# Pair attention: ScalarE's adds of two slots issued ahead of the next block's exponential, with another choice of ScalarE's five halves

## The chip, the cores and the metric

The kernel runs on one core of a Trainium2 chip. The time is the device time of one execution in microseconds (us). Before the change the median of three runs is 5141.64 us, and the runs lie between 5141.53 and 5143.81 us.

Five engines of the core matter here. TensorE (PE in the profile) multiplies matrices. VectorE (DVE), ScalarE (ACT) and GpSimd (POOL) work on elements. SyncE (SP) issues most of the transfers. Each engine takes its instructions strictly in the order in which the program lists them, and waits for the others through semaphores.

## What is computed

Two layers are computed one after the other, each an attention and a feed-forward network (FFN) with residuals and normalisation. The change touches the attention of the second layer alone. In the reference it is this:

```python
q = jnp.einsum('bnc,ac->bna', X, Wq)
k = jnp.einsum('bnc,ac->bna', X, Wk)
Vy = jnp.einsum('bnc,dc->bnd', X, Wy_w) + Wy_b
e = jax.nn.relu(_rho_signed_sqrt(q[:, :, None, :] + k[:, None, :, :]))
scores = jnp.einsum('bija,a->bij', e, Wphi)
m = jnp.max(scores, axis=-1, keepdims=True)
ex = jnp.exp(scores - m)
denom = jnp.sum(ex, axis=-1)
part1 = jnp.einsum('bij,bjc->bic', ex, Vy)
Ew = jnp.einsum('bij,bija->bia', ex, e)
part2 = jnp.einsum('bia,ca->bic', Ew, We_w) + We_b * denom[..., None]
```

The quantity `e`, which has an element for each query, key and one of 64 channels, is the large one. The relu of the signed root keeps only the root of the positive part, so the kernel computes it as a relu of the sum `q + k` and then a square root. It is needed twice, once for the scores and once more, weighted by `ex`, for `Ew`.

## The kernel before

**The tiling.** There are 4 batches of 1024 tokens. The queries are taken 32 at a time, which makes a *block*; there are 128 blocks (`N = B * NB`). A block consists of 8 *pairs*, numbered 0 to 7, and a pair of two *halves*, so that half i = 2 * pair + h runs from 0 to 15. One half is a tile of 128 partitions x 1024 keys. A pair is one buffer `s` of 128 x 2048, taken from a ring of 14 buffers (`RING`).

**What is done to a pair.** First each half gets its add: `max(k + q, 0)`. This is done on one of three engines: GpSimd for the halves in `ADD_ON_POOL` (line 1381, issued by `begin`), ScalarE for the halves in `RELU_ON_SCALAR` (line 1403, in `pair`), and VectorE for the others (line 1392, in `adds`). Then ScalarE takes the square root of the whole pair in place (line 1404), and TensorE adds the pair into the block's scores with 32 products (line 1408). When all 8 pairs are in, `top` takes a maximum on VectorE (line 1418), `quarters` (line 1420) and two products (line 1421) spread it, `exps` takes the final maximum on VectorE (`neg`, line 1425), and ScalarE computes the exponential (line 1427). `spread` copies the weights to all partitions with TensorE (line 1434, tile `xb`). At last VectorE multiplies each half by its weights and sums it, in `weigh` (line 1454); only then is the ring buffer free.

**The order.** It is written out by hand. The main loop goes over the blocks n and, inside, over 8 *steps* p. In step p VectorE weighs the two halves of pair p of block n, with the add of a pair that is 12 pairs ahead in between. After that come `top` of block n+1 (step 5), or `exps` and the first `spread` of block n+1 (step 6). Then `work` issues a share of other work, namely the first layer's remainder at the start, and later the second layer's FFN. At the end of the step a pair 14 ahead is begun (GpSimd's add) and a pair 12 ahead is made (`make`, which calls `pair`). So the step decides which pair is made:

| step p | pair made, of block n+2 (n+1 for p below 4) | ScalarE's halves before | VectorE's half before |
|---|---|---|---|
| 0 | 4 | 8 | - |
| 1 | 5 | - | 10 |
| 2 | 6 | 12 | - |
| 3 | 7 | 14 | 15 |
| 4 | 0 | - | 0 |
| 5 | 1 | 2 | - |
| 6 | 2 | - | 4 |
| 7 | 3 | 6 | 7 |

GpSimd has halves 1, 3, 5, 9, 11 and 13. So each engine's number of halves of a block is fixed: five on ScalarE, five on VectorE and six on GpSimd. While the first layer's remainder still runs (`first_rest`), the ring lends a buffer to it, and everything is one pair less ahead.

ScalarE must load another function table whenever it goes from the square root to the exponential and back. The FFN's own SiLU and GELU passes (line 1357, `between` and `switch`) are held back until directly after the exponential, so that they share a change of table. Their normalisation (lines 913 and 929, in `normed`) runs wherever `work` issues it.

Of the kernel before, what the change touches and what calls it, by code (L numbers as in the profile page):

```python
# [8 lines left out]
AF = mybir.ActivationFunctionType  # L9
# [22 lines left out]
PREP = 12  # L32
ROOM = (4, 6, 6, 6, 6, 4, 3, 6)
LATE = 2
RELU_ON_SCALAR = (2, 6, 8, 12, 14)
FIRST_ON_SCALAR = 6
ADD_ON_POOL = (1, 3, 5, 9, 11, 13)
LEAD = 2
# [5 lines left out]
@with_exitstack  # L44
def block_kernel(ctx: ExitStack, tc: tile.TileContext, a, out):
    nc = tc.nc
    keep = ctx.enter_context(tc.tile_pool(name="keep", bufs=1))


    kept = ctx.enter_context(tc.tile_pool(name="kept", bufs=1, space=DRAM))  # L50
    link = {
        "x1": [kept.tile([U, C], F32, tag=f"x1_{j}", name=f"x1_{j}") for j in range(B * T // U)],
        "x2": [kept.tile([FB, C], F32, tag=f"x2_{j}", name=f"x2_{j}") for j in range(B * T // FB)],
        "gates": [kept.tile([1, 2, B, C], F32, tag=f"gates{j}", name=f"gates{j}") for j in range(2)],
        "brow": kept.tile([1, C], F32, tag="brow", name="brow"),
        "yg": kept.tile([P, 4, U], F32, tag="yg", name="yg"),
        "qd": kept.tile([T, 64], F32, tag="qd0", name="qd0"),
        "kd": kept.tile([8, P, T], F32, tag="kd0", name="kd0"),
        "vd": kept.tile([T, C + 1], F32, tag="vd0", name="vd0"),
    }  # L60

    ident = keep.tile([P, P], F32, tag="ident", name="ident")
    nc.scalar.dma_start(ident, a["ident"])
    eps = keep.tile([P, 3], F32, tag="eps", name="eps")
    for i, v in enumerate((EPS_LN, EPS_GN, EPS_RHO)):
        nc.vector.memset(eps[:, i : i + 1], v)
    cols = [keep.tile([P, 6, 2, B], F32, tag=f"mcols{i}", name=f"mcols{i}") for i in range(2)]
    seen = keep.tile([P, NE], F32, tag="seen", name="seen")
    link["qt"] = [keep.tile([P, 64, 8], F32, tag=f"qt{i}", name=f"qt{i}") for i in range(2)]
    nc.gpsimd.memset(seen, 0.0)  # L70
    first_layer(tc, a, link, cols, seen, ident, eps)
    pair_attention(tc, a, link, out, cols, seen, ident, eps)
# [750 lines left out]
def pair_attention(tc, a, link, out, cols_of, seen, ident, eps):  # L823
# [10 lines left out]
    nc = tc.nc  # L834
    NB = T // 32
# [3 lines left out]
    with tc.tile_pool(name="at_k", bufs=1) as pk, tc.tile_pool(name="at_w", bufs=1) as wp, tc.tile_pool(  # L839
# [14 lines left out]
        kB, qtab, kds, vds = {0: {}}, {0: link["qt"][0]}, {0: link["kd"]}, {0: link["vd"]}  # L854
# [18 lines left out]
        for i in range(2):  # L873
            t = wp.tile([P, 4, P], F32, tag=f"ewt{i}", name=f"ewt{i}")
            nc.gpsimd.memset(t, 0.0)
            ewt.append(t)
            t = wp.tile([P, 4, 64], F32, tag=f"ew{i}", name=f"ew{i}")
# [379 lines left out]
        def follower():  # L1257

            return groups.get(stream[1]) if len(stream) > 1 else None
# [103 lines left out]
        class Block:  # L1363


            def __init__(self, n):
                self.n, self.b, self.s, self.added = n, n // NB, {}, set()
                self.sc = psc.tile([P, 512], F32, tag="sc", name="sc")

            def on_scalar(self, i):  # L1370
                return i in RELU_ON_SCALAR if self.n else i < FIRST_ON_SCALAR

# [3 lines left out]
            def begin(self, p):  # L1376
                self.s[p] = ring.tile([P, 2, T], F32, tag="s", name="s")
                for h in range(2):
                    i = 2 * p + h
                    if self.n and i in ADD_ON_POOL:  # L1380
                        nc.gpsimd.tensor_scalar(  # L1381
                            self.s[p][:, h, :], kB[self.b][i % 8], self.query(i), 0.0, ALU.add, ALU.max
                        )

            def adds(self, p):
# [3 lines left out]
                for h in range(2):  # L1389
                    i = 2 * p + h  # L1390
                    if not (self.n and i in ADD_ON_POOL or self.on_scalar(i)):
                        nc.vector.tensor_scalar(  # L1392
                            self.s[p][:, h, :], kB[self.b][i % 8], self.query(i), 0.0, ALU.add, ALU.max
                        )

            def pair(self, p):
                t = self.s[p]
                s = p // 4
                self.adds(p)
                for h in range(2):  # L1400
                    i = 2 * p + h
                    if self.on_scalar(i):
                        nc.scalar.activation(t[:, h, :], kB[self.b][i % 8], AF.Relu, bias=self.query(i))  # L1403
                nc.scalar.activation(t, t, AF.Sqrt, bias=eps_rho)  # L1404
                for h in range(2):
                    g = (2 * p + h) % 8
                    for j in range(4):
                        nc.tensor.matmul(  # L1408
                            self.sc[32 * j : 32 * j + 32, 0:256],
                            wsel[:, g, 16 * (1 - s) : 16 * (1 - s) + 32],  # L1410
                            t[:, h, 256 * j : 256 * (j + 1)],
                            start=p == 0 and h == 0,
                            stop=p == 7 and h == 1,
                        )
# [121 lines left out]
        N = B * NB  # L1536
        blocks = {0: Block(0)}
        begun = made = 0
# [3 lines left out]
        def work(room):  # L1542


            tick()
            turns[0] += 1
            if issues and turns[0] % 2:
                issues.pop(0)()
            for of in (tasks, stream):
                while of and room > 0:  # L1550
                    got = next(of[0], self_done)
                    if got is self_done:
                        of.pop(0)
                    elif got is None:
                        break
                    else:
                        room -= got
# [10 lines left out]
        def make():  # L1568
            nonlocal made
            n, p = made // 8, made % 8  # L1570
            if n < N:
                blocks[n].pair(p)
                if n % NB == NB - 1 and n + 1 < N and p >= 4:
                    for g in range(2 * p - 8, 2 * p - 6):
                        spread_keys(n // NB + 1, g)
            made += 1
# [13 lines left out]
        for n in range(N):  # L1590
            cur = blocks.pop(n)
            ew = ews[n // 4 % 2]
            if n % 4 == 0:
                exT = p2.tile([P, 4, 2, P], F32, tag="exT", name="exT")
            nxt = n + 1 < N
            if n % NB == PREP and n // NB + 1 < B:
                stream.insert(min(1 + (follower() in heads), len(stream)), prepare(n // NB + 1))
            for p in range(8):
                if p == 0:
                    cur.spread(1)  # L1600
                    cur.turn()
                if p == 2:
                    cur.turned(exT)
                cur.weigh(p, 0, ew)
                if made < 8 * N:
                    blocks[made // 8].adds(made % 8)
                cur.weigh(p, 1, ew)
                if nxt and p == 5:
                    blocks[n + 1].top()
                if nxt and p == 6:  # L1610
                    blocks[n + 1].exps()
                    blocks[n + 1].spread(0)
                work(ROOM[p])
                while begun <= 8 * n + p + ahead[0]:
                    begin()
                    make()
            if n % 4 == 3:
                tasks.append(finish(n, ew, exT))
# [104 lines left out]
```

## Time and profile before

| | |
|---|---|
| median of the three runs | 5141.64 us |
| the profiled execution, its own time | 5137.34 us |
| its span, first to last instruction | 5135.6 us |
| mean granted TensorE clock | 0.900 |
| first and last exponential of the attention (line 1427) start at | 1268.9 and 4968.3 us |
| GpSimd's adds (line 1381) | 762 x 3.792 us |
| VectorE's adds (line 1392) | 645 x 0.922 us |
| VectorE's weighing (line 1454) | 2048 x 1.209 us |
| scores on TensorE (line 1408) waiting for the square root, matmul rows | 402.5 us |
| VectorE's score maximum (line 1418) waiting for TensorE | 208.8 us |
| VectorE's weighing waiting for the spread weights (line 1434) | 33.7 us |

"Span" is the time between the first and the last instruction of the profiled execution; the execution's own time holds 1.7 us more. Durations are those of this one execution. The pages of the profile give, for each group of instructions, the busy time, the mean duration of one, and the idle time of the engine just in front of it with what ended it. Passes of ScalarE and VectorE overlap their predecessor by a little under 0.1 us, so starts, not durations, are subtracted where a rate is wanted.

The 128 exponentials divide the attention into 127 intervals. From block 28 on most of them fall into a pattern of eight that returns, because two groups of the FFN take eight blocks; eight copies of it run from block 28 to 51, 68 to 83 and 100 to 123. The copy from 4203.1 us (block 100) to 4430.5 us (block 108) is the one used for working things out.

### The profile page before, as it was taken

Reading aid. Unit: us, or ns where it says so; the run is one execution under the profiler, and the core shown is the slowest. Engines: PE = TensorE matmul, PEld = TensorE weight load, DVE = VectorE, ACT = ScalarE, POOL = GpSimd, SP = SyncE. Lnnn points to the kernel's source line nnn. Section 1 sums busy time; section 2 is a strip of 40 time slices with the busy share of each in tenths; the row PEclk is TensorE's granted clock in tenths of the full one; section 3 lists DMA queues with packets and bytes.
Section 4 is the critical chain, followed back from the end, with each engine's and each line's share of the span. In section 5 each row is a group of like instructions: output and inputs, shape, how many; then the busy total and the mean of one; then the engine's idle time right before and its main releaser. Section 6 shows DMA issues by size and latency. Waiting matters only on the chain.

```text
span 5135.6 us, 75609 instructions
## 1 busy us (share of the span) xinstructions
PE 4334.1 (84%) x28714; PEld 2437.5 (47%) x28714; DVE 4175.7 (81%) x7255; ACT 3690.1 (72%) x3438; POOL 3396.9 (66%) x1233
## 2 busy tenths in 40 slices
PE   6788888877688979888887988888889889798888
PEld 2233333333234635555554555555455556455557
DVE  5877777765799888888888888888888988988871
ACT  2322222213899889999998889999888999999961
POOL 3533343433688777787887778788867877887840
PEclk8798888988798989999898999999889999999999
DMA  4233333344011222222121323222223222121223
GB/s 137 85 101 105 96 97 89 88 115 117 18 36 58 82 86 87 98 74 83 61 73 51 118 76 111 69 78 71 72 72 108 99 77 80 62 79 66 73 82 114
DMA packets 255787, 429.16 MB, mean 84 GB/s; under 512 B 71752, under 2 KB 142592, under 8 KB 255168
## 3 DMA queue, kind: packets, MB, share of 16 engines
q1 hardware_dynamic: 251776, 420.76, 25.8%
q8 instruction: 227, 3.72, 0.3%
q10 hardware_dynamic: 3168, 1.99, 0.1%
q0 software_dynamic: 480, 1.57, 0.1%
q14 instruction: 136, 1.11, 0.1%
HBM read 396.13 MB, written 40.67 MB: 85 GB/s over the span
## 4 chain that ended last, share of the span: by engine, by line
PE 34%; ACT 18%; DVE 15%; issue 7%; POOL 1%; DMA 0%; ACTq 0%; POOLq 0%; SPq 0%; DVEq 0%
PE ff_ps L1315 14%; PE sc L1408 10%; DVE s L1454 9%; ACT s L1404 9%; ACT s L1403 4%; PE xb L1434 2%; DVE s L1392 2%; PE out_ps L1336 2%; PE o L1505 2%; ACT L1404 2%; ACT L1357 1%; PE o L1517 1%; PE ff_ps L1245 1%; ACT wide L1357 1%; ACT ex L1427 1%
## 5 line engine op out<-in xcount | busy, mean ns | idle before, releaser
L1381 POOL TENSOR_SCALAR s<-kB,qt 128x1024 f32<-128x1024 f32 x762 | 2879.7, 3792 | 603.6 <-DVE ew L1454 480.4
L1454 DVE CUSTOM_DVE_ANT_0 s<-s,xb 128x1024 f32<-128x1024 f32 x2048 | 2417.0, 1209 | 35.1 <-PE xb L1434 33.7
L1404 ACT ACTIVATE s<-s,eps 128x2048 f32<-128x2048 f32 x1024 | 2027.6, 2000 | 76.0 <-DVE s L1392 30.4
L1408 PE MATMUL sc<-s,wsel 128*32 128x256 f32 x16384 | 1198.5, 417 | 404.6 <-ACT s L1404 402.5
L1315 PE MATMUL ff_ps<-wide,fw 128*128 128x256 f32 x4096 | 1006.0, 395 | 29.2 <-ACT wide L1357 25.6
L1408 PEld LDWEIGHTS sc<-s,wsel 128*32 128x32 f32 x16384 | 456.2, 115 | 1006.9 <-ACT s L1404 600.3
L1315 PEld LDWEIGHTS ff_ps<-wide,fw 128*128 128x128 f32 x4096 | 765.7, 194 | 237.6 <-issue 99.5
L1403 ACT ACTIVATE s<-kB,qt 128x1024 f32<-128x1024 f32 x641 | 728.9, 1138 | 23.5 <-DMA yg<-out_g 22.8
L1392 DVE TENSOR_SCALAR s<-kB,qt 128x1024 f32<-128x1024 f32 x645 | 594.1, 922 | 0.4 <-DMA kB<-kd 0.4
L729 POOL TENSOR_TENSOR kv<-vb,out_k 128x512 f32<-128x512 f32 x256 | 323.1, 1270 | 285.5 <-DVE state L797 225.5
L607 PE MATMUL e_ps<-wd,hid 128*128 128x512 f32 x896 | 429.1, 626 | 34.0 <-DVE acc L590 33.2
L1434 PE MATMUL xb<-ex,pick 64*128 64x256 f32 x2048 | 324.9, 440 | 56.9 <-ACT ex L1427 56.9
L797 DVE TENSOR_TENSOR_SCAN state<-dec,carry,kv 128x512 f32<-128x512 f32 x256 | 325.9, 1273 | 9.9 <-POOL carry L792 5.0
L607 PEld LDWEIGHTS e_ps<-wd,hid 128*128 128x128 f32 x896 | 176.0, 202 | 281.0 <-issue 273.4
L1434 PEld LDWEIGHTS xb<-ex,pick 64*128 64x128 f32 x2048 | 195.4, 206 | 194.6 <-ACT ex L1427 96.8
L1245 PE MATMUL ff_ps<-wide,fw 128*128 128x256 f32 x1024 | 266.0, 409 | 6.1 <-ACT wide L929 5.8
L799 DVE TENSOR_TENSOR pr<-state,rec 128x512 f32<-128x512 f32 x256 | 176.0, 687 | 113.2 <-ACT state L795 66.5
L789 ACT COPY carry<-state 128x1 f32<-128x1 f32 x255 | 47.8, 187 | 263.9 <-DVE state L797 262.9
L1245 PEld LDWEIGHTS ff_ps<-wide,fw 128*128 128x128 f32 x1024 | 197.4, 202 | 64.9 <-issue 25.3
L1418 DVE TENSOR_REDUCE sc<-sc 128x1 f32<-128x256 f32 x128 | 54.9, 429 | 208.9 <-PE sc L1408 208.8
L1299 DVE TENSOR_TENSOR wide<-ff_ps,ffn_s 128x512 f32<-128x512 f32 x128 | 87.7, 685 | 167.7 <-PE ff_ps L1315 167.7
L1427 ACT ACTIVATE ex<-sc,neg 128x256 f32<-128x256 f32 x128 | 60.6, 473 | 201.0 <-DVE neg L1425 200.1
(254 smaller groups left out, 4002.8 us busy)
## 6 DMA issues: line engine op xcount, KB each, us to landing
fw<-in_ffw_dram SPq DMA_DIRECT2D x354, 512.0 KB
vb<-vd SPq DMA_DIRECT2D x1024, 64.0 KB
lent<-vd SPq DMA_DIRECT2D x64, 514.0 KB
wd<-in_w_down_dram SPq DMA_DIRECT2D x28, 1024.0 KB
kB<-kd SPq DMA_DIRECT2D x32, 512.0 KB
lent<-in_We_dram SPq DMA_DIRECT2D x32, 512.0 KB
kd<-nd SPq DMA_DIRECT2D x24, 512.0 KB
vd<-out_v SPq DMA_DIRECT2D x8, 512.0 KB
```

The costliest lines, as they stand in the source:

```text
L607: nc.tensor.matmul(ps, hid[:, k, t * P : (t + 1) * P], wd[:, k, :], start=k == 0, stop=k == HID // P - 1)
L729: nc.gpsimd.tensor_mul(kv, vb[:, g % 2, :], ready[u]["k"][:, n // HN, :])
L797: nc.vector.tensor_tensor_scan(s[:, 1 : U + 1], dec, kv, c, ALU.mult, ALU.add)
L1245: nc.tensor.matmul(ps[:, h, :], w[:, k, o : o + P], hT[:, k, :], start=k == 0, stop=k == 1)
L1315: nc.tensor.matmul(ps[:, h, :], w[:, k * P : (k + 1) * P], of[:, k, :], start=k == 0, stop=k == 7)
L1381: nc.gpsimd.tensor_scalar(self.s[p][:, h, :], kB[self.b][i % 8], self.query(i), 0.0, ALU.add, ALU.max)
L1392: nc.vector.tensor_scalar(self.s[p][:, h, :], kB[self.b][i % 8], self.query(i), 0.0, ALU.add, ALU.max)
L1403: nc.scalar.activation(t[:, h, :], kB[self.b][i % 8], AF.Relu, bias=self.query(i))
L1404: nc.scalar.activation(t, t, AF.Sqrt, bias=eps_rho)
L1408: nc.tensor.matmul(self.sc[32 * j : 32 * j + 32, 0:256], wsel[:, g, 16 * (1 - s) : 16 * (1 - s) + 32], t[:, h, 256 * j : 256 * (j + 1)], s ...
L1434: nc.tensor.matmul(xb[:, 256 * j : 256 * (j + 1)], pick[q, j % 2, s, :], self.ex[q, :], start=True, stop=True)
L1454: nc.vector.tensor_tensor_reduce(t[:, h, :], t[:, h, :], self.xb[s], 1.0, 0.0, ALU.mult, ALU.add, ew[:, self.n % 4, col : col + 1])
```

## The change

There are two edits. The first replaces the five halves that ScalarE adds: 2 and 6 leave the list, 4 and 7 enter it. VectorE takes 2 and 6 instead of 4 and 7, since it takes whatever neither of the others has. The second splits ScalarE's adds of a pair off into a function `relus`, which does them once, and calls it in step 6 for the pairs that are begun and not yet made, in front of `exps`. In the steady state those are the pairs made in steps 6 and 7, that is, halves 4 and 7; `pair` later finds them done.

```diff
-RELU_ON_SCALAR = (2, 6, 8, 12, 14)
+RELU_ON_SCALAR = (4, 7, 8, 12, 14)
...
+            def relus(self, p):
+                if p in self.relued:
+                    return
+                self.relued.add(p)
+                for h in range(2):
+                    i = 2 * p + h
+                    if self.on_scalar(i):
+                        nc.scalar.activation(self.s[p][:, h, :], kB[self.b][i % 8], AF.Relu, bias=self.query(i))
+
             def pair(self, p):
                 t = self.s[p]
                 s = p // 4
                 self.adds(p)
-                for h in range(2):
-                    i = 2 * p + h
-                    if self.on_scalar(i):
-                        nc.scalar.activation(t[:, h, :], kB[self.b][i % 8], AF.Relu, bias=self.query(i))
+                self.relus(p)
                 nc.scalar.activation(t, t, AF.Sqrt, bias=eps_rho)
...
                 if nxt and p == 6:
+                    for m in range(made, min(begun, 8 * N)):
+                        blocks[m // 8].relus(m % 8)
                     blocks[n + 1].exps()
                     blocks[n + 1].spread(0)
```

More of the change, by code (lines that the diff above doesn't have):

```diff
@@ L1366, in __init__ @@
             def __init__(self, n):
-                self.n, self.b, self.s, self.added = n, n // NB, {}, set()
+                self.n, self.b, self.s, self.added, self.relued = n, n // NB, {}, set(), set()
                 self.sc = psc.tile([P, 512], F32, tag="sc", name="sc")
```

## The prediction

> **What bounds the kernel now.** I read the page's busy shares and chain first, then its groups, then the waits of the exponential, then single blocks in order of time.
>
> ```profile
> PE 4334.1 (84%) x28714; PEld 2437.5 (47%) x28714; DVE 4175.7 (81%) x7255; ACT 3690.1 (72%) x3438; POOL 3396.9 (66%) x1233
> ...
> PE 34%; ACT 18%; DVE 15%; issue 7%; POOL 1%; DMA 0%; ACTq 0%; POOLq 0%; SPq 0%; DVEq 0%
> ```
>
> No engine is the bound. The chain that ended last changes engines: it runs on TensorE while the FFN's products fill it, on VectorE, and on ScalarE after an exponential. In the attention ScalarE is the fullest: from 2000 to 2500 us it is busy 455.5 of 500 us (TensorE 437, VectorE 435). What it still idles is mostly one wait:
>
> ```profile
> L1404 ACT ACTIVATE s<-s,eps 128x2048 f32<-128x2048 f32 x1024 | 2027.6, 2000 | 76.0 <-DVE s L1392 30.4
> ...
> L1403 ACT ACTIVATE s<-kB,qt 128x1024 f32<-128x1024 f32 x641 | 728.9, 1138 | 23.5 <-DMA yg<-out_g 22.8
> ...
> L1427 ACT ACTIVATE ex<-sc,neg 128x256 f32<-128x256 f32 x128 | 60.6, 473 | 201.0 <-DVE neg L1425 200.1
> ```
>
> The last row: 201 us idle in front of the exponential, in 78 of the 128 blocks; in the other 50 ScalarE came late itself. The wait is uneven: along the eight-block pattern (exponentials 101 to 108) it is 0, 2.07, 3.95, 0.47, 0, 4.64, 0 and 0 us. The change fills this hole. What counts is whether it was on the path, and what the filling does where there is no hole.
>
> **The change on ScalarE.** The adds are five per block before and after. Up to now, from exponential to exponential, ScalarE does roots 2, add 6, 3, add 8, 4, 5, add 12, 6, add 14, 7, 0, add 2, 1. Afterwards: roots 2, 3, add 8, 4, 5, add 12, 6, add 14, 7, 0, 1, then adds 4 and 7. By starts: root to root 1.91 us (4211.11 to 4213.02), root-add-root 3.07 (4204.90 to 4207.97) to 3.14, so an add between roots costs 1.16 to 1.23. Two adds in a row before the table load cost an estimated 1.04 each (1.13 less the 0.09 overlap). Hence: (a) 0.3 us less of ScalarE per block; (b) everything from root 3 to root 0 comes 1.16 us sooner after the exponential, root 1 by 2.4; (c) from root 1 to the exponential there are 2.1 us more, or 0.86 more counted from root 0.
>
> **The change on VectorE.** Its five adds stay, but one moves: half 4's in step 6, between score maximum and `neg`, goes; half 2's comes in step 5, ahead of the maximum. Where VectorE waits there for scores, the new add is free and the old one (0.67 to 1.6 us) leaves the path to `neg`. Otherwise they cancel. And root 1, which needed only ScalarE and GpSimd, now waits for VectorE's step 5. A block where this bites, ScalarE first, then VectorE:
>
> ```profile
> 4309.11 2.00 ACT L1404 ACTIVATE s<-s,eps 128x2048 f32<-128x2048 f32 x1 [1.05 <-DVE s L1392]
> 4311.02 1.13 ACT L1403 ACTIVATE s<-kB,qt 128x1024 f32<-128x1024 f32 x1
> 4312.24 2.00 ACT L1404 ACTIVATE s<-s,eps 128x2048 f32<-128x2048 f32 x1
> 4314.26 1.28 ACT L1427 ACT_TABLE_LOAD   x1
> 4316.01 0.47 ACT L1427 ACTIVATE ex<-sc,neg 128x256 f32<-128x256 f32 x1 [0.47 <-DVE neg L1425]
> ```
>
> ```profile
> 4310.07 1.21 DVE L1454 CUSTOM_DVE_ANT_0 s<-s,xb 128x1024 f32<-128x1024 f32 x1
> ...
> 4311.21 1.21 DVE L1454 CUSTOM_DVE_ANT_0 s<-s,xb 128x1024 f32<-128x1024 f32 x1
> ...
> 4312.35 0.42 DVE L1418 TENSOR_REDUCE sc<-sc 128x1 f32<-128x256 f32 x1
> ...
> 4314.02 0.75 DVE L1392 TENSOR_SCALAR s<-kB,qt 128x1024 f32<-128x1024 f32 x1
> ...
> 4315.82 0.15 DVE L1425 TENSOR_REDUCE neg<-sc 128x1 f32<-128x4 f32 x1
> ```
>
> The new add fits in at 4311.21 and ends at 4311.96. Root 1, two adds, load: 0.06 + 1.91 + 1.04 + 1.15 + 1.30 = 5.46, so the exponential could start at 4317.4 instead of 4316.01. `neg` stays (one add in, one out). The exponential is 1.4 to 1.6 us late, and what is queued behind it on ScalarE is late too: the FFN's wide pass and root 2, for which TensorE waits.
>
> **The table load against a rule.** The rows show 1.28 us, starting 0.02 after the pass in front, with the next pass 0.01 behind. [...]
>
> **GpSimd.**
>
> ```profile
> 4365.73 7.37 POOL L1381 TENSOR_SCALAR s<-kB,qt 128x1024 f32<-128x1024 f32 x2
> 4377.98 3.70 POOL L1381 TENSOR_SCALAR s<-kB,qt 128x1024 f32<-128x1024 f32 x1 [4.88 <-DVE ew L1454]
> ```
>
> The second pass of the first row is half 9 and ends at 4373.1, before pair 6 is weighed (4374.8): it took the buffer of pair 5. So a buffer goes to whichever pair is first written. With add 7 in front, pair 3 takes that buffer and half 9 waits for pair 6's: from 4369.4 to 4374.8. It then ends at 4378.5, root 4 needs it at about 4381.7; halves 11 and 13 follow at 4382.2 and 4385.9, and root 6 comes at 4387.0 (4388.18 less 1.16). The narrowest margin is 1.1 us, so I cost it at nothing; without it, root 6 waits for the excess. VectorE's moved add runs more often beside GpSimd (97% of blocks there, 81% before; adds beside it average 0.97 us, others 0.75). Bounds of an add: 0.74 to 1.70; I take 0.95. TensorE's products, the transfers and SP's queue are the same in number and order.
>
> **The sum for eight blocks** (shift of the path, us):
> - 100 to 101: ScalarE never idles: -0.3.
> - 101 to 102: root 2, TensorE, then VectorE to `neg`; add 0.95 for 0.70: +0.25. The 2.07 wait just holds two adds.
> - 102 to 103: TensorE throughout: 0. The 3.95 us hole is filled for nothing.
> - 103 to 104, 105: +1.5 as above. TensorE later waited 0.72 for root 7, which now comes sooner, so +0.8 remains.
> - 105 to 106: TensorE, then VectorE's maximum after 2.65 us of waiting; the add behind it (1.59 long) goes: -1.5.
> - 106 to 107: ScalarE again: -0.3.
> - 107 to 108: the path comes by the FFN's normalisation, which ScalarE ends at 4426.04. Then add, root, load was 4.55 to the exponential; root, add, add, load is 5.40: +0.86.
>
> That is -0.2 in 227 us, or -1.5 for the eight copies. By the same steps 60 to 68 and 92 to 100 give -0.5, -0.7, -0.3, -0.7, +1.0, thus -1.2 each; 12 to 27, 52 to 59 and 84 to 91 about +1 (five times -0.7 and five times -0.3 against 1.6, 0.6 and four times 0.86); the first eleven blocks -0.3 each, -3 (an add out of the run up to the last root, 1.16, one in before `neg`, 0.75 to 0.95). Together -6 us. The profiled execution's 5137.3 becomes 5131; the median stands 4.3 above it, so **5136 us** is forecast: gains and losses cancel. About 0.2%, 10 us, is what a measurement tells from no change.
>
> **Rivals.**
> - *The hole was on the path.* Then each waiting block gains up to one add: the smaller of 1.13 and its wait sums to 78 us. For it: 50 of the 78 waits are on the chain. Against: after the longest waits the chain goes on over TensorE, where an earlier root 3 buys nothing. 50/78 of it is 50 us: 5092.
> - *The exponential becomes the late one (slower).* Place: blocks in which VectorE reaches the maximum without waiting. I count 32 whose step-5 add then decides, 34 us of lateness, and nine behind the normalisation, 9 us. Price: all of it on the path, less 19 us of adds gone in front of `neg`: 5166. It decides from about 1.3 us of lateness on: after `neg` VectorE has 2.9 us of weighing and adding, exponential and spread take 1.6. For it: roots for which TensorE waits 402 us stand right behind. Against: VectorE has waited only 33.7 us for spread weights.
> - *GpSimd turns late.* Its FFN additions (1.27 and 0.73 us) stand in the same queue, and 1.1 us is little. Half a microsecond in 60 blocks: 5172. Against: ScalarE has waited 1.3 us for it in all.
>
> **Chances.** Cancelling 0.44, hole on the path 0.24, late exponential 0.25, GpSimd 0.07. Cancelling has its own range, 5115 to 5160: the add's bounds give 8 cycles x 2 places x (-0.2 to +0.75), thus -3 to +12, and 0.1 us in the spacing of adds over some 75 blocks 8 either way. Of its 0.44, 0.28 lies within 10 us, 0.09 below and 0.07 above. So faster 0.33, same 0.28, slower 0.39. The range 5100 to 5178 reaches into the first rival and over most of the others.
>
> **What would show it.** The wait for `neg` falls from 201 to under 100 us, ScalarE's adds go on at 641, and its busy time hardly moves. Exponentials like 104 start over 1 us behind `neg`; VectorE's wait for `xb` rises from 33.7 to 60 or so; the 208.8 us wait of the maximum shrinks, being filled by the new add. GpSimd's third pass of a run starts right after pair 6 is weighed. If `xb` waits rise beyond 100 us, the second rival holds; if ScalarE's roots wait for GpSimd for tens of us, the third; if intervals 100 to 101 and 103 to 104 both shorten by over 1 us, the first.

## The result, and the profile after

The changed kernel takes 5184.60 us in the median of four runs (5178.51 to 5191.88), beside 5141.59 us for the kernel before (5138.86 to 5143.81): a ratio of 1.0084, with a 95% interval of 1.0067 to 1.0102. It is slower by 43 us, where 5136 us and a range up to 5178 us were forecast. The profiled execution took 5186.07 us, with a span of 5184.3 us.

First the page of the changed kernel: busy time, the chain, and the groups that answer to those shown of before.

```profile
PE 4379.9 (84%) x28714; PEld 2471.1 (48%) x28714; DVE 4192.6 (81%) x7255; ACT 3681.8 (71%) x3438; POOL 3382.1 (65%) x1233
...
PE 39%; ACT 17%; DVE 14%; issue 5%; POOL 1%; DMA 1%; SPq 0%; POOLq 0%; ACTq 0%; DVEq 0%
...
L1460 DVE CUSTOM_DVE_ANT_0 s<-s,xb 128x1024 f32<-128x1024 f32 x2048 | 2421.4, 1211 | 91.7 <-PE xb L1440 68.3
L1410 ACT ACTIVATE s<-s,eps 128x2048 f32<-128x2048 f32 x1024 | 2014.9, 1998 | 179.5 <-DVE s L1392 144.3
...
L1403 ACT ACTIVATE s<-kB,qt 128x1024 f32<-128x1024 f32 x641 | 718.0, 1137 | 23.7 <-DVE acc L590 22.7
...
L1424 DVE TENSOR_REDUCE sc<-sc 128x1 f32<-128x256 f32 x128 | 54.5, 426 | 146.3 <-PE sc L1414 117.9
```

The exponential's row of the same kernel, from the groups kept by line (the last figures are idle time and what ended it):

```profile
L1433 ACT ACTIVATE ex<-sc,neg 128x256 f32<-128x256 f32 x128 | 60.6, 474 | 99.8 <-DVE neg L1431 98.8
```

ScalarE did the same work; its waiting moved. The wait in front of the exponential fell from 201.0 to 99.8 us, and that in front of the roots rose from 76.0 to 179.5, of which VectorE's adds end 144.3 (30.4 before). Nearly all of it is root 1's: counted by the order of the roots in a block, waits of over 0.15 us in front of root 1 make 103.3 us, where they made 1.3. So ScalarE won nothing in sum. VectorE's wait for the spread weights doubled, from 33.7 to 68.3 us.

Where this happens is seen in one block. ScalarE, from root 0 to the exponential 107 of the pattern, then VectorE, then TensorE:

```profile
4423.46 1.99 ACT L1410 ACTIVATE s<-s,eps 128x2048 f32<-128x2048 f32 x1
4426.95 2.00 ACT L1410 ACTIVATE s<-s,eps 128x2048 f32<-128x2048 f32 x1 [1.51 <-DVE s L1392]
4428.86 2.17 ACT L1403 ACTIVATE s<-kB,qt 128x1024 f32<-128x1024 f32 x2
4431.05 1.28 ACT L1433 ACT_TABLE_LOAD   x1
4432.34 0.47 ACT L1433 ACTIVATE ex<-sc,neg 128x256 f32<-128x256 f32 x1
```

```profile
4425.38 1.47 DVE L1392 TENSOR_SCALAR s<-kB,qt 128x1024 f32<-128x1024 f32 x1
...
4427.91 0.42 DVE L1424 TENSOR_REDUCE sc<-sc 128x1 f32<-128x256 f32 x1
...
4430.73 0.15 DVE L1431 TENSOR_REDUCE neg<-sc 128x1 f32<-128x4 f32 x1
...
4435.10 1.22 DVE L1460 CUSTOM_DVE_ANT_0 s<-s,xb 128x1024 f32<-128x1024 f32 x1 [1.28 <-PE xb L1440]
```

```profile
4432.87 2.08 PE L1440 MATMUL xb<-ex,pick 64*128 64x256 f32 x8 [1.83 <-ACT ex L1433]
```

VectorE's step-5 add (half 2) ends at 4426.85, and root 1, which waited 1.51 us for it, starts at 4426.95. Root, two adds and load take 5.39 us, so the exponential starts at 4432.34, which is 1.46 behind `neg`. The spread lands 2.76 us after the exponential's start, and VectorE, out of work at 4433.82, waits 1.28 us for it. That delays its next step-5 add. So there is a loop from VectorE over root 1, the two adds, the load, the exponential and the spread back to VectorE. Before the change root 1 had no link to VectorE's step 5. The time by which an exponential starts behind the end of its `neg` is called its *lateness* from here on. Over the 128 blocks it is over 1 us in 66 instead of 7, and 118 instead of 40 us in sum.

The intervals between the exponentials of the pattern, from starts in the traces (us). The first column of figures is the interval before the change, the others are differences from it; the last column belongs to a run told of below:

| interval | before | forecast | changed | changed, add half a step sooner |
|---|---|---|---|---|
| 100 to 101 | 26.22 | -0.3 | -0.23 | -0.35 |
| 101 to 102 | 31.71 | +0.25 | +0.68 | +0.78 |
| 102 to 103 | 28.65 | 0 | +0.46 | +1.77 |
| 103 to 104 | 26.33 | +1.5 | +1.54 | +0.45 |
| 104 to 105 | 29.44 | -0.7 | -0.14 | -0.34 |
| 105 to 106 | 29.43 | -1.5 | -1.19 | -1.32 |
| 106 to 107 | 24.71 | -0.3 | +1.27 | +0.18 |
| 107 to 108 | 30.89 | +0.86 | +2.33 | +0.59 |
| sum | 227.38 | -0.2 | +4.7 | +1.8 |

The eight copies of the pattern are 36.7 us longer together, of 51 us between the first and the last exponential of these two executions; where the other 14 us arise was not followed. Summed over the eight copies, three of the eight places make all of the 36.7: 103 to 104 with 12.6 us, 106 to 107 with 10.2 and 107 to 108 with 14.9. The other five cancel.

### The profile page after: what moved, and what is told of

Same layout as the page of the kernel before. It is cut to its first block, busy times and chain, and to the rows that moved or that the text cites. A ratio compares the mean times of both kernels' runs of the same rounds, so it can differ in the third digit from the quotient of the medians.

```text
span 5184.3 us, 75627 instructions
## 1 busy us (share of the span) xinstructions
PE 4379.9 (84%) x28714; PEld 2471.1 (48%) x28714; DVE 4192.6 (81%) x7255; ACT 3681.8 (71%) x3438; POOL 3382.1 (65%) x1233
## 4 chain that ended last, share of the span: by engine, by line
PE 39%; ACT 17%; DVE 14%; issue 5%; POOL 1%; DMA 1%; SPq 0%; POOLq 0%; ACTq 0%; DVEq 0%
PE ff_ps L1315 15%; PE sc L1414 11%; DVE s L1460 8%; ACT s L1410 7%; ACT s L1403 3%; PE xb L1440 3%; DVE s L1392 3%; PE out_ps L1336 2%; PE o L1511 2%; ACT L1410 1%; ACT L1433 1%; PE ff_ps L1245 1%; ACT wide L1357 1%; ACT L1357 1%; PE o L1523 1%
## 5 line engine op out<-in xcount | busy, mean ns | idle before, releaser
L1381 POOL TENSOR_SCALAR s<-kB,qt 128x1024 f32<-128x1024 f32 x762 | 2865.0, 3772 | 661.3 <-DVE ew L1460 233.1
L1460 DVE CUSTOM_DVE_ANT_0 s<-s,xb 128x1024 f32<-128x1024 f32 x2048 | 2421.4, 1211 | 91.7 <-PE xb L1440 68.3
L1410 ACT ACTIVATE s<-s,eps 128x2048 f32<-128x2048 f32 x1024 | 2014.9, 1998 | 179.5 <-DVE s L1392 144.3
L1414 PE MATMUL sc<-s,wsel 128*32 128x256 f32 x16384 | 1201.8, 420 | 322.1 <-ACT s L1410 321.5
L1403 ACT ACTIVATE s<-kB,qt 128x1024 f32<-128x1024 f32 x641 | 718.0, 1137 | 23.7 <-DVE acc L590 22.7
L1392 DVE TENSOR_SCALAR s<-kB,qt 128x1024 f32<-128x1024 f32 x645 | 606.3, 941 | 0.1
```

The source lines that it names most:

```text
L1381: nc.gpsimd.tensor_scalar(self.s[p][:, h, :], kB[self.b][i % 8], self.query(i), 0.0, ALU.add, ALU.max)
L1392: nc.vector.tensor_scalar(self.s[p][:, h, :], kB[self.b][i % 8], self.query(i), 0.0, ALU.add, ALU.max)
L1403: nc.scalar.activation(self.s[p][:, h, :], kB[self.b][i % 8], AF.Relu, bias=self.query(i))
L1414: nc.tensor.matmul(self.sc[32 * j : 32 * j + 32, 0:256], wsel[:, g, 16 * (1 - s) : 16 * (1 - s) + 32], t[:, h, 256 * j : 256 * (j + 1)], s ...
L1460: nc.vector.tensor_tensor_reduce(t[:, h, :], t[:, h, :], self.xb[s], 1.0, 0.0, ALU.mult, ALU.add, ew[:, self.n % 4, col : col + 1])
```

## The experiments

Three theories. **A**: root 1's new wait for VectorE's step-5 add closes the loop above. **B**: the adds in front of the exponential make it late, whatever root 1 waits for. **C**: GpSimd's half 9, which gets a later buffer, and VectorE's adds that run beside GpSimd's passes make the difference. Each diff is against the changed kernel unless it says otherwise; ratios are to the kernel before, with their 95% interval.

### The two parts apart

The choice of halves alone, against the kernel before:

```diff
-RELU_ON_SCALAR = (2, 6, 8, 12, 14)
+RELU_ON_SCALAR = (4, 7, 8, 12, 14)
```

> Only the choice of halves is changed (ScalarE 4, 7, 8, 12, 14; VectorE 2 and 6); ScalarE's adds stay directly in front of their roots. Root 1 waits for VectorE's step-5 add as in the changed kernel (its idle time at VectorE's adds 100 us or more instead of 30), but no add stands between root 1 and the table load. Theory A, the closed loop of VectorE's add, root 1, two adds, load and exponential: without the two adds the loop is 2.1 us shorter, so most of the loss goes: 5138 to 5158 us. Theory B, the two adds in front of the exponential are late whatever root 1 waits for: 5132 to 5146. Theory C, GpSimd's half 9 that gets a later buffer, and VectorE's add that collides with it: the buffers go as before, so 5136 to 5146. Under all three it is clearly below the changed kernel's 5185; at 5175 or more the choice alone does it and A's adds don't matter.

5213.35 us, 1.0142 (1.0126 to 1.0157). All three theories missed: the choice alone costs 73 us. The exponential is hardly ever late (15.0 us of lateness in sum, 39.9 before), but the five adds 4, 7, 8, 12 and 14 now all stand between it and root 7. From the exponential to root 7 it takes 19.59 us instead of 18.42 (means of blocks 27 to 122), one add in full; from root 7 to the next exponential 9.97 instead of 10.55.

The early adds alone, with the old halves:

```diff
-RELU_ON_SCALAR = (4, 7, 8, 12, 14)
+RELU_ON_SCALAR = (2, 6, 8, 12, 14)
```

> Only the early adds, with the old halves (2, 6, 8, 12, 14): one add, half 6, stands in front of the exponential, root 1 has its ScalarE add and waits for no VectorE add. The buffers change hands as in the changed kernel. Theory A: no loop through VectorE, 5130 to 5148. Theory B: half of the loss, 5155 to 5170. Theory C: nearly the whole loss, 5165 to 5190, with GpSimd's adds idling near 660 us as in the changed kernel and ScalarE's roots or VectorE's adds later for it.

5151.57 us, 1.0021 (1.0012 to 1.0029): 11 us, between A and B and far from C. With one add moved from behind the exponential to its front, those two stretches are 17.70 and 11.37 us: what one gives, the other takes. VectorE waits 58.9 us for the spread weights here, nearly as long as in the changed kernel, so the size of that wait alone does not tell the loss.

Half 4 alone early, then half 7 alone:

```diff
-                    for m in range(made, min(begun, 8 * N)):
+                    for m in range(made, min(begun, made + 1, 8 * N)):
```

> The changed kernel with half 4's add alone in front of the exponential; half 7's goes back in front of root 3. So one ScalarE add stands between root 7 and the exponential and four between the exponential and root 7, as before the change, and what differs from before is that root 1 waits for VectorE's step-5 add. The buffers change hands as before the change. Theory A, the wait of root 1 costs by itself: about the 33 us between the changed kernel and the one with the add a step earlier, 5160 to 5178. Theory B, only the number of adds on either side of the exponential counts: 5134 to 5148. Theory C, only GpSimd's later buffer counts: 5134 to 5148.

```diff
-                    for m in range(made, min(begun, 8 * N)):
+                    for m in range(made + 1, min(begun, 8 * N)):
```

> The changed kernel with half 7's add alone in front of the exponential; half 4's goes back in front of root 2. The same count of adds on either side as with half 4 alone, the same wait of root 1, but pair 3 is now written before half 9, so GpSimd's half 9 gets the later buffer. Theory A: within 6 us of the kernel with half 4 alone, 5158 to 5182. Theory B: 5134 to 5150. Theory C: at least 15 us above the kernel with half 4 alone.

With half 4 alone 5136.11 us, 1.0006 (0.9994 to 1.0017): no difference from before. With half 7 alone 5211.56 us, 1.0140 (1.0122 to 1.0157). Their pages, half 4 first:

```profile
L1410 ACT ACTIVATE s<-s,eps 128x2048 f32<-128x2048 f32 x1024 | 2025.2, 1999 | 130.2 <-DVE s L1392 89.1
L1414 PE MATMUL sc<-s,wsel 128*32 128x256 f32 x16384 | 1193.5, 416 | 334.8 <-ACT s L1410 332.5
```

```profile
L1410 ACT ACTIVATE s<-s,eps 128x2048 f32<-128x2048 f32 x1024 | 2013.3, 1998 | 169.9 <-DVE s L1392 134.9
L1414 PE MATMUL sc<-s,wsel 128*32 128x256 f32 x16384 | 1210.8, 422 | 375.1 <-ACT s L1410 374.6
```

The first is what B and C expected, and not A; the second is what C expected, and neither A nor B. Two things follow. Root 1's wait (78.4 of the 89.1 us) costs little while one add stands behind it: A in its first form, in which the wait costs by itself, falls. What is left of A is a second, strict form: the wait costs where two adds and the load stand behind root 1. And the 73 us of the choice come from half 4's add standing behind the exponential, in front of root 2; put in front of the exponential, and nothing else changed, it pays them back. With half 7 in its place TensorE waits 42 us longer for the roots (374.6 against 332.5), though that sum is no measure of the loss: it was 402.5 before the change, and is 321.5 in the changed kernel and 450.2 with the choice alone. The 75 us more are what C expected, but the copies below show that the buffer alone isn't the cause. Half 7 early gains nothing on the choice alone (1.0140 against 1.0142). In this order, the change is +73 (choice), about -70 (half 4 early) and +40 (half 7 early, with half 4 early already). It is the last 40 that have to be explained. Why an add in front of root 2 costs so much more than one in front of root 3 was not followed further.

### Root 1's wait

The add of half 2 a whole step earlier, then half a step:

```diff
                 cur.weigh(p, 1, ew)
+                if p == 4 and made + 1 < min(begun, 8 * N):
+                    blocks[(made + 1) // 8].adds((made + 1) % 8)
```

> The changed kernel, and VectorE's add of half 2 is issued one step earlier, at the end of step 4. Both adds still stand in front of the exponential. Theory A: root 1 no longer waits for VectorE (its idle time at VectorE's adds falls from 144 to below 30 us), the lateness of the exponential behind its maximum falls by more than half, and the time to 5135 to 5155. Theory B: ScalarE's queue is as long as before, 5172 to 5190. Theory C: the half 2 add avoids half 9's pass at least in part but GpSimd keeps its later buffer, 5165 to 5185.

```diff
+                if p == 5 and made < 8 * N:
+                    blocks[made // 8].adds(made % 8)
                 cur.weigh(p, 0, ew)
```

> The changed kernel, with VectorE's add of half 2 at the start of step 5, in front of the first weighing instead of between the two: 1.14 us sooner, and not a whole step as in the run with the add at the end of step 4. Theory A: root 1's idle time at VectorE's adds between 69 and 144 us, and the time between those two kernels, 5150 to 5174. Theory C: the buffers stay as they are, 5176 to 5190.

The whole step gave 5151.70 us, 1.0024 (1.0014 to 1.0034), the time that A expected and not B's or C's. The waits fell less than A said: ScalarE's at VectorE's adds from 144.3 to 68.7 us, where below 30 was expected (root 1's own from 103.3 to 24.7), and the lateness from 118 to 88 us in sum, not by half. Half a step gave 5144.93 us, 1.0005 (0.9995 to 1.0015), below the 5150 to 5174 that A expected: 40 of the 43 us are gone, with both adds still in front of the exponential and GpSimd's buffers as in the changed kernel. B and C have no place for that. Nor has TensorE's clock. With the change its mean granted clock fell from 0.900 to 0.884 and its busy time rose from 4334.1 to 4379.9 us; the half step has the same clock, 0.884, and the same busy time without the loss, and the choice alone loses its 73 us at 0.900. The half step's page, with the busy times and the roots' row, and the same block on ScalarE and on VectorE:

```profile
PE 4381.0 (85%) x28714; PEld 2472.8 (48%) x28714; DVE 4193.4 (81%) x7255; ACT 3678.3 (71%) x3438; POOL 3421.4 (66%) x1233
...
L1410 ACT ACTIVATE s<-s,eps 128x2048 f32<-128x2048 f32 x1024 | 2011.0, 1997 | 100.7 <-DVE s L1392 66.3
```

```profile
4397.38 2.00 ACT L1410 ACTIVATE s<-s,eps 128x2048 f32<-128x2048 f32 x1 [0.42 <-DVE s L1392]
4399.29 2.17 ACT L1403 ACTIVATE s<-kB,qt 128x1024 f32<-128x1024 f32 x2
4401.48 1.28 ACT L1433 ACT_TABLE_LOAD   x1
4402.77 0.47 ACT L1433 ACTIVATE ex<-sc,neg 128x256 f32<-128x256 f32 x1
```

```profile
4395.76 1.53 DVE L1392 TENSOR_SCALAR s<-kB,qt 128x1024 f32<-128x1024 f32 x1
...
4402.29 0.16 DVE L1431 TENSOR_REDUCE neg<-sc 128x1 f32<-128x4 f32 x1
...
4405.54 1.22 DVE L1460 CUSTOM_DVE_ANT_0 s<-s,xb 128x1024 f32<-128x1024 f32 x1
```

The add has one weighing less in front of it, root 1 waits 0.42 instead of 1.51 us (29.0 instead of 103.3 in all blocks), the exponential is 0.32 behind `neg` instead of 1.46, and VectorE's next weighing starts after a gap of 0.15 us instead of a wait of 1.28. In the table the intervals 103 to 104, 106 to 107 and 107 to 108 give back 1.1, 1.1 and 1.7 us; 102 to 103 takes 1.3 of them. Over the eight copies these three are 4.1, 1.5 and 8.3 us longer than before instead of 12.6, 10.2 and 14.9.

The same two moves with half 4 alone early, and the whole step with the choice alone:

> Half 4's add alone in front of the exponential, and VectorE's add of half 2 one step earlier: the same count of adds on either side as before the change, no wait of root 1 for the step-5 add, the buffers as before. Theories A and B both: the time of before, 5132 to 5148, perhaps some us less for one add that no longer stands between two roots. If it stays above 5155, neither the wait nor the count of adds explains the changed kernel.

> Half 4 alone in front of the exponential, with the same move of half 2's add to the start of step 5. Theory A says that here root 1's wait costs next to nothing, so nothing is to be had: 5130 to 5148; the whole step cost 20 us, with VectorE's adds at 1032 ns instead of 990, so if the collision with GpSimd's passes counts, the adds' mean decides: above 1010 ns 5145 to 5160. If root 1's wait still costs, 5110 to 5128.

> Only the choice of halves, with no early add, and VectorE's add of half 2 one step earlier. Five adds stand between the exponential and root 7, none between root 7 and the exponential. If the wait of root 1 costs its 31 to 33 us here too, 5172 to 5188, with what remains above before coming from the fifth add behind the exponential. If the wait only bites when adds and a load stand behind root 1 (the loop of Theory A taken strictly), it stays at 5203 to 5220.

Half 4 with the whole step: 5156.28 us, 1.0040 (1.0026 to 1.0054), a miss for A and B; with half a step: 5131.44 us, 0.9979 (0.9968 to 0.9990), the fastest with the new choice, and 0.2% faster than the kernel before. The choice alone with the whole step: 5218.81 us, 1.0160 (1.0141 to 1.0179), so there the wait was not the cause, as the strict form of A has it. By what was expected of the first of these, it leaves the changed kernel unexplained. But the half step opens root 1's wait as far (17.5 us, 18.3 with the whole step) and costs nothing, so the 17 us above half 4 alone (1.0040 against 1.0006) are a price of the whole step itself; from what they come is open. Half a step against the unmoved add is thus worth 40 us with two adds behind root 1, and some 14 with one (0.9979 against 1.0006). So up to 14 of the 40 us need no second add.

### Half 2 left with ScalarE

```diff
-RELU_ON_SCALAR = (4, 7, 8, 12, 14)
+RELU_ON_SCALAR = (2, 4, 7, 12, 14)
```

> The changed kernel with halves 2, 4, 7, 12, 14 on ScalarE: half 2 stays with ScalarE, as before the change, and VectorE takes half 8 in step 0 for it. Two adds stand in front of the exponential as in the changed kernel, but root 1 waits for no VectorE add, and the stretch from root 0 to the exponential is one add longer than in the changed kernel. Theory A: the loop is open, 5140 to 5165. Theory B: the adds in front of the exponential remain and one more stands close to it, 5180 to 5205. Theory C: the buffers are as in the changed kernel, 5175 to 5190.

5217.09 us, 1.0150 (1.0135 to 1.0166): a miss for A, and more than B and C said. The edit brought root 1's wait down to 1.6 us and made others: root 0 waits 68 us and root 5 for half 10 56 us, since ScalarE, with fewer adds behind the exponential, comes to them sooner, while the exponential's lateness grows to 221 us in sum. It opened one link and made others, so it can't tell the theories apart; A's forecast for it stays a miss.

### GpSimd's later buffer

A copy of one column makes pair 3's first write come before half 9's, once in the kernel with half 4 alone early and once in the kernel before (there into half 6):

```diff
+                    if made + 1 < min(begun, 8 * N):
+                        nc.scalar.copy(blocks[(made + 1) // 8].s[(made + 1) % 8][:, 1, 0:1], eps_rho)
                     blocks[n + 1].exps()
```

> The kernel with half 4 alone in front of the exponential (5136 us), and in front of the exponential a copy of one column by ScalarE into half 7 of pair 3, which its add overwrites later. It makes pair 3's first write come before half 9's, so that GpSimd's half 9 gets the later buffer, as in the changed kernel, at the price of some 0.2 us of ScalarE a block instead of a second add. Theory A, in its second form (root 1's wait for VectorE costs only where two adds and the load stand behind it): 5133 to 5150. Theory C (GpSimd's later buffer makes the difference between one early add and two): 5158 to 5182, with GpSimd's idle time in front of its adds mostly after the weighing of pair 6.

> The kernel before the change with the same copy of one column, into half 6 of pair 3, in front of the exponential: the old halves, no early add, only the later buffer for half 9. Theory A: the time of before plus at most the copy, 5130 to 5147. Theory C: 5150 to 5185.

5152.75 us, 1.0027 (1.0017 to 1.0038), some 11 us more than without the copy and between what A and C expected (up to 5150, from 5158); and 5128.25 us, 0.9977 (0.9966 to 0.9989), 12 us less than before, a little under the 5130 to 5147 that A expected and far from C's 5150 and more. With half 4 alone early and the copy, GpSimd waits as was meant: of its idle time in front of these adds 236.3 us are put down to the weighing, as in the changed kernel (233.1), instead of 513.5 without the copy. The later buffer takes a little in one kernel and gives as much in the other: by itself it is not what costs 40 us.

### The rate of the spread

In the block shown the spread's products take 2.08 us. At exponential 101 of the changed kernel, where TensorE came to them without a wait, they take 1.14:

```profile
4260.03 1.14 PE L1440 MATMUL xb<-ex,pick 64*128 64x256 f32 x8
```

Filler products (zero weights, so the scores stay) were put into TensorE's idle time in front of the quarters and of the spread, in the changed kernel and in the one before; first in every block of two kinds, then in the pattern's 16 such blocks only.

```diff
+                if nxt and p in (5, 6) and made > 8 * (n + 2) and (n + 1) % 8 in (0, 3):
+                    nought = wsel.rearrange("p g c -> p (g c)")[:, 32:64]
+                    for i in range(16):
...
```

> The changed kernel; in the blocks whose exponential is number 0 or 3 of each eight (104 and 107 of the pattern) 16 products with zero weights are added to the scores in step 5, in front of the quarters' products, and 16 in step 6, in front of the spread. They fill TensorE's idle 1.2 and 1.8 us there. Theory A with a slow spread: the spread behind these exponentials takes 1.1 to 1.3 us instead of 2.08, VectorE's wait for the spread weights falls by some 20 us, and the time to 5150 to 5173. If the rate of the spread is no part of it: 5182 to 5205, the fillers being work on top.

> The kernel before the change with the same 32 filler products in the same blocks. Theory A: the exponentials 104 and 107 come 0.03 and 0.57 us behind their maximum there, so a faster spread brings at most some 10 us, 5122 to 5145. If a warmer TensorE speeds the whole attention by itself, it gains as much as the changed kernel does, 20 us or more: below 5120.

> The changed kernel with the filler products in the blocks of the eight-block pattern only (28 to 51, 68 to 83, 100 to 123; exponentials 0 and 3 of each eight, 16 blocks in all). If the slow spread carries a part of the loss: 5162 to 5175, that is 10 to 20 us below the changed kernel, a ratio to the kernel before of 1.004 to 1.0065. If what was seen in those stretches was chance: 5180 to 5190, a ratio of 1.0075 or more.

> The kernel before the change with the fillers in the same 16 blocks. Its exponentials there are hardly late, so the faster spread brings little: ratio 0.998 to 1.001. If the fillers help by warming TensorE for the other products too, they bring as much here as in the changed kernel: 0.9975 or less.

The first pair gave 5190.56 us, 1.0104 (1.0091 to 1.0118), for the changed kernel and 5162.63 us, 1.0051 (1.0038 to 1.0065), for the one before, where at most 5145 was expected: outside the pattern the fillers are work on top. The second pair gave 5184.93 us, 1.0083 (1.0069 to 1.0097), and 5133.28 us, 0.9996 (0.9987 to 1.0005). Both times of the changed kernel are what was expected if the slow spread carries no part of the loss. The fillers did what they should, here behind exponential 107 of the changed kernel with fillers in the pattern:

```profile
4437.23 1.14 PE L1440 MATMUL xb<-ex,pick 64*128 64x256 f32 x8
```

In the 16 blocks the spread takes 1.13 us instead of 2.08, and VectorE's wait behind it falls from 1.30 to 0.55 us in the mean. The interval 107 to 108 shortens from 33.22 to 31.47, while 103 to 104 and 106 to 107 stay at 27.88 and 25.98. Over the eight copies, 107 to 108 is 5.5 us longer than before the change instead of 14.9, the other two stay at 12.6 and 10.2, and the eight copies take 1847.2 us instead of 1859.1. In the kernel before, the fillers move the same sum by 0.7 us (1821.7 for 1822.4).

So the loss in the pattern has two parts. Root 1's wait puts 103 to 104 and 106 to 107 back directly, and a faster spread doesn't touch that. The way back through the spread to VectorE costs in 107 to 108, and there the faster products take off 9.4 us of 14.9, most of the 12 by which the eight copies are shorter in this execution. The whole time doesn't show these 12 us (1.0083 against 1.0084, in intervals some 15 us wide). In the execution with the fillers the attention's first exponential also comes 7.7 us later than in the changed kernel's, at 1273.9 for 1266.2 us, a start that lies between 1262.3 and 1281.5 us in the profiled executions of all these kernels. How much of the loss in the whole time the slow spread carries thus stays open.

## Why the prediction was wrong

- **ScalarE's durations and the table load: right.** In the block shown the load takes 1.28 us; it starts 0.02 us after the last add, and the exponential 0.01 after the load. Interval 100 to 101 of the copy worked out changed by -0.23 (forecast -0.3), and the late exponentials come 1.46 us behind `neg` (forecast 1.4 to 1.6).
- **VectorE's add at 0.95 us: right** (mean 0.941). So was its add's going from in front of `neg` in 105 to 106: -1.19 for -1.5.
- **GpSimd at nothing: right enough.** The roots wait 4.4 us for it, and the copies above moved the time by 11 and -12 us.
- **The step that failed is the sum's treatment of root 1's wait.** "And root 1, which needed only ScalarE and GpSimd, now waits for VectorE's step 5" was seen, and priced in one interval of eight, 103 to 104, where "+0.8 remains". The 106 to 107 interval was put down as "ScalarE again: -0.3", because ScalarE had no idle time there before. With the new link that interval follows VectorE: root 1 waits 1.51 us, and it is +1.27. In 107 to 108, +0.86 became +2.33, and of the 1.54 in 103 to 104 only 0.14 came back. Over the eight copies, 103 to 104 itself came out as forecast, 12.6 us for 12; but 104 to 105 gave back 0.6 for 5.6, 106 to 107 is +10.2 for -2.4, and 107 to 108 +14.9 for +6.9. These are 26 of the 38 us by which the pattern missed its forecast. Moving that one add by one weighing, 1.14 us, took 40 of the 43 us away.
- **The slack was mis-sized.** The rival of the late exponential "decides from about 1.3 us of lateness on", from 2.9 us of VectorE's work less 1.6 for exponential and spread. The 2.9 is right (2.94 in the block shown). From the exponential's start to the weighing that needs the spread it is 2.76 us, since the eight products take 2.08 us there and not 1.14. That leaves 0.18 us. The trace of before had it in the very block that the prediction shows:

```profile
4316.54 2.08 PE L1434 MATMUL xb<-ex,pick 64*128 64x256 f32 x8 [0.31 <-ACT ex L1427]
```

The 1.4 to 1.6 us of lateness that were forecast for this block lay over the 1.3 already, so by the prediction's own figures VectorE would have had to wait. Two adds behind root 1 give 1.46 of lateness, one gives 0.42 (exponentials 104 and 107 of the kernel with half 4 alone), and half a step leaves 0.32 to 0.41: this goes with 43, 3 and 3 us of loss, by the ratios. The fillers show that the duration of the spread alone isn't it.
- **Of the rivals, the late exponential held**, with 5166 us priced too low: the credit of adds gone in front of `neg` came in, but the delay came back through VectorE, in 107 to 108 most of all. The mark that was set for it was too high: the wait for `xb` went to 68.3 us, not beyond 100, though the whole idle time of the weighing went to 91.7.
- **That the hole was on the path** is refuted: in the changed kernel 201 us of waiting became 99.8 at no gain, and with the half step, at the time of before, they became 145.7 at no gain either.

## What to carry to other kernels

When work is moved between engines, list for every consumer which engine it waits for now that it did not wait for before, and follow that link once around the loop: a new link can make an interval that one engine filled without idling follow another. Price the slack of a loop from the rows of the blocks where it closes, with the durations that stand there (2.08 us for the spread here, and not the 1.14 of exponential 101). And a moved operation is best tried part by part: half 4 early pays 70 us, half 7 early on top of it costs 40 (and without it nothing), and the place of one add within its step is worth another 40.

## What was not expected of the hardware

- **TensorE's rate behind idle time.** The same eight spread products took 2.08 us in all 16 blocks of the kind of 104 and 107 in the changed kernel's pattern, behind waits of 1.82 to 1.93 us; 1.14 at exponential 101, where TensorE came without a wait; and 1.13 in the same 16 blocks with fillers in the waits: a ratio of 1.8. The wait just in front doesn't settle it: before the change they took 2.08 us behind a wait of 0.31 at exponential 104, and 1.13 behind one of 1.34 at 102. What sets the rate is not shown here. The mean granted clock rose from 0.884 to 0.898 with the fillers in 16 blocks, and the whole time stayed.
- **VectorE's adds beside GpSimd's passes.** In the trace of the changed kernel the 601 adds of VectorE that overlap one of GpSimd's in time took 955 ns in the mean, the other 44 took 749. All 645 took 922 ns in the mean before the change and 875 ns with the copy of one column, which is there only to shift GpSimd's passes:

```profile
L1392 DVE TENSOR_SCALAR s<-kB,qt 128x1024 f32<-128x1024 f32 x645 | 563.7, 875 | 0.0
```

That is 30 us of VectorE's time, in a kernel that is 0.23% faster. But it can't be called the source of the gain: with half 4 alone early the same copy took the mean from 990 to 933 ns, and that kernel became 11 us slower. Nor does the mean tell why half a step did better than a whole one (946 against 974 ns with both adds early, 1012 against 1032 with half 4 alone). For a mean above 1010 ns, 5145 to 5160 us were expected of half 4 alone with half a step, if these collisions decide; its mean is 1012, and it took 5131.44. What these longer adds cost stays open.
